# Selective scan on one core: products with C for two directions in one instruction, u for four rows, part of B's diagonals on GpSimd

## The chip, the cores and the metric

The kernel runs on one core of a Trainium2 chip. The core has five engines that run side by side, each with its own queue that it works through in order: TensorE (PE in the profile, with its weight loads as PEld), VectorE (DVE), ScalarE (ACT), GpSimd (POOL) and SyncE (SP, which here only issues transfers). The metric is the device time of one execution in microseconds (us), the median of several runs.

## The reference

Four layers are added to an image of 56 x 56 points with 128 channels, four images one after the other: a window attention layer with global attention and an MLP, a selective scan layer, a deformable convolution, and the first kind again. The change is in the second layer, whose core is a scan over the 3136 points in four orders (by rows, by columns, and both backwards), with 256 channels and 16 states for each channel:

```
def step(h, inp):
    u_i, d_i, b_i, c_i = inp
    dA = jnp.exp(d_i[..., None] * A)
    h = h * dA + (d_i * u_i)[..., None] * b_i[:, None, :]
    y = jnp.einsum('gdn,gn->gd', h, c_i)
    return (h, y)
...
x_t = jnp.transpose(xa, (0, 2, 1, 3)).reshape(b, L, D_INNER)
xs = jnp.stack([x_flat, x_t, jnp.flip(x_flat, 1), jnp.flip(x_t, 1)], axis=1)
...
dts4, Bp4, Cp4 = (rep4(dts), rep4(Bp), rep4(Cp))
```

The step sizes d, and B and C, are the same for the four directions at the same step number; only u differs. The four results are brought back to the image's order and added up.

## The kernel before

`run` takes the images in turn; for each, `mamba` first makes the convolved input `xa` and writes the step sizes and the rows of B and C to memory (`mamba_conv`), then runs `mamba_scan`, and then normalises, gates and projects (`mamba_out`). The change is inside `mamba_scan` alone, which stands four times in the span.

A **unit** of the scan is one line of 56 points in one direction, for 128 channels (half `j` of the 256) and all 16 states. On VectorE it is one scan instruction over 16 x 58 = 928 elements, where the two leading columns of every state carry the end of the line before. Units run in the order `(g, r, d)`: `g = 2s + j` is a pair of lines `s` for one half of the channels, `r` is the line in the pair, `d` the direction. There are 56 x 2 x 4 = 448 units in an image; eight units share a `g`.

Around each scan stand these steps, all recorded in an order written out by hand (`manual_schedule`): a loop over `u` (L1116) issues the fixed steps of each unit, and two lists, `soon` and `plan`, hold what `at(t, f)` has put at unit `t`. Each engine works its own instructions off in that order.

- `chunk` (L899): every 32 units, loads of step sizes and rows of B and C for four lines, 32 units ahead, and a split of the rows into a rounded part and a remainder.
- `mult` (L991): u times step size, `du`, on GpSimd, one instruction for each direction and two lines (112 elements).
- `high`, `low`, `low2` (L1004 to L1014): `du` in a rounded part (twice) and its remainder (twice), `dh`; ScalarE copies, GpSimd subtracts.
- `turn` and `keep` (L1016, L1021): TensorE transposes `dh`, ScalarE copies the result to `ut` (7 tiles).
- `b_rows` and `b_diag` (L943, L950): TensorE transposes the rows of B, VectorE spreads them along a diagonal mask into `dgb`, for one half line of 28 points (448 elements) in each instruction. The transposed rows lie in PSUM.
- `inputs` (L1041): TensorE multiplies `ut` with `dgb` into `dbu` in PSUM (2 buffers), one unit ahead of its scan.
- `zero` and `decays` (L996, L1000): the factors `da`; `inject` (L1057) and `save` (L1068): ScalarE copies the carry into `dbu` before a scan and out of `hs` after it.
- `scan` (L1061) writes `hs`; a tile `hs` holds two directions of one line, and there are three tiles.
- `c_spread` and `c_out` (L959, L970): C on all partitions, `cb`, for two lines.
- `weigh` (L1072): GpSimd multiplies `hs` by `cb` in place, one unit after the scan (896 elements).
- `add_up` (L1077): TensorE transposes the product and sums over the states, three units after the scan; `sum_out` (L1091): ScalarE copies a pair's sums to `ys` (6 tiles).
- `back` and `back_add` (L1095, L1102): TensorE turns the sums back, VectorE adds them to `ya`, at 14, 15 and 16 units from the start of the eight.

The order inside one unit `u` is: `save(u-1)`, `inputs(u+1)`, what `soon` holds, `weigh(u-1)`, `scan(u)`, `inject(u+1)`, `add_up(u-3)`, `sum_out` on every odd unit, and what `plan` holds.

Of the kernel before, what the change touches and what calls it, by code (L numbers as in the profile page):

```python
# [19 lines left out]
P = 128  # L20
HW = 56
# [19 lines left out]
NST = 16  # L41
SC = 224
# [36 lines left out]
class _Net:  # L79
# [795 lines left out]
    def mamba_scan(self, b, xa, ya, s1):  # L875
# [10 lines left out]
        with tc.tile_pool(name="ms", bufs=2) as sb, tc.tile_pool(name="ms_ps", bufs=2, space=PSUM) as ps, tc.manual_schedule():  # L886
# [6 lines left out]
            def at(t, f, plan=plan):  # L893
                plan.setdefault(t, []).append(f)
# [41 lines left out]
            def rows(s):  # L936

                m = made["r", s] = {}
                first = 16 * s
                src = made["c", s // 2]  # L940
                where = (s % 2) * 2 * HW

                def b_rows(r):  # L943
                    m["pb"] = bank("pbt")
                    for tb in range(2):
                        nc.tensor.transpose(
                            m["pb"][:TK, tb * NX : (tb + 1) * NX], src["xs"][:, (s % 2) * 4 + 2 * r + tb].rearrange("k g t -> k (g t)"), self.ident[:NX, :NX]
                        )

                def b_diag(r, tb):  # L950
                    t = m[r, tb] = sb.tile([TK, NST, TB], F32R, tag="dgb", name="dgb", bufs=8)
                    nc.vector.tensor_tensor(
                        t,
                        m["pb"][:TK, tb * NX + DTR : tb * NX + DTR + NST][:, :, None].to_broadcast([TK, NST, TB]),
                        dmask[:, None, :].to_broadcast([TK, NST, TB]),
                        ALU.mult,
                    )
# [12 lines left out]
                def c_out(k):  # L970
                    nc.scalar.copy(m["cb"][:, 4 * k : 4 * k + 4, :].rearrange("p n t -> p (n t)"), m.pop(("pc", k))[:, : 8 * HW])

                for r in range(2):
                    t = first - 16 + 8 * r
                    at(t, lambda r=r: b_rows(r))
                    for tb in range(2):
                        at(t + 1 + tb, lambda r=r, tb=tb: b_diag(r, tb))
                for k, t in enumerate((-10, -9, -2, -1)):
                    at(first + t + 1, lambda k=k: c_out(k))
                    at(first + t, lambda k=k: c_spread(k))  # L980

            def inputs_of(g):

                s, j = divmod(g, 2)
                m = made[g] = {}
                first = 8 * g - 15
                src = made["c", s // 2]
                dl = lambda: src["dl"][:, j, (s % 2) * 2 * HW : (s % 2 + 1) * 2 * HW].rearrange("p (r t) -> p r t", t=HW)
                flat = lambda t: t.rearrange("p d s g t -> p (d s) g t")

                def mult(d):  # L991
                    if d == 0:
                        m["du"] = sb.tile([P, 4, 2 * HW], F32, tag="du", name="du", bufs=1)
                    nc.gpsimd.tensor_tensor(m["du"][:, d, :].rearrange("p (r t) -> p r t", t=HW), dl(), self.direction(xa[:, j, :], d, 2 * s, 2), ALU.mult)

                def zero():  # L996
                    m["da"] = sb.tile([P, 2, NST, RW], F32, tag="da", name="da", bufs=3)
                    nc.gpsimd.memset(m["da"][:, :, :, 0:2], 0.0)

                def decays(n):  # L1000
                    for n in (n, n + 1):
                        nc.scalar.activation(m["da"][:, :, n, 2:], dl(), AF.Exp, scale=A[:, j, n : n + 1])  # L1002

                def high():  # L1004
                    m["dh"] = sb.tile([P, 4, 4, 4, TB], F32R, tag="dh", name="dh", bufs=1)
                    du = m["du"].rearrange("p d (s t) -> p (d s) t", t=TB)
                    nc.scalar.copy(flat(m["dh"])[:, :, 0:2, :], du[:, :, None, :].to_broadcast([P, 16, 2, TB]))

                def low():
                    du = m["du"].rearrange("p d (s t) -> p (d s) t", t=TB)  # L1010
                    nc.gpsimd.tensor_tensor(flat(m["dh"])[:, :, 2, :], du, flat(m["dh"])[:, :, 0, :].bitcast(F32), ALU.subtract)

                def low2():
                    nc.scalar.copy(flat(m["dh"])[:, :, 3, :], flat(m["dh"])[:, :, 2, :].bitcast(F32))  # L1014

                def turn(i):  # L1016
                    m["pt", i] = bank("pt")
                    for d in range(4):
                        nc.tensor.transpose(m["pt", i][:TK, d * P : (d + 1) * P], m["dh"][:, d, i].bitcast(F32).rearrange("p g t -> p (g t)"), self.ident)

                def keep(i):  # L1021
                    m["ut", i] = sb.tile([TK, 4, P], F32R, tag="ut", name="ut", bufs=7)
                    nc.scalar.copy(m["ut", i].rearrange("k d c -> k (d c)"), m.pop(("pt", i))[:TK, :])

                for d in range(4):
                    at(first + d, lambda d=d: mult(d))
                at(first + 4, zero)
                for i in range(8):
                    at(first + 5 + i, lambda i=i: decays(2 * i), soon)
                at(first + 5, high)  # L1030
                at(first + 6, low)
                at(first + 8, low2)
                for i in range(4):
                    at(first + 10 + i, lambda i=i: keep(i))
                    at(first + 9 + i, lambda i=i: turn(i))
# [5 lines left out]
            def inputs(u):  # L1041
                g, r, d = units[u]

                pu = ps.tile([P, 1024], F32, tag="dbu", name="dbu")
                pu = pu[:, 512 - UW // 2 : 512 + UW // 2].rearrange("p (n t) -> p n t", n=NST)
                for tb in range(2):
                    for h in range(2):
                        nc.tensor.matmul(  # L1048
                            pu[:, 8 * h : 8 * h + 8, 2 + tb * TB : 2 + (tb + 1) * TB],
                            lhsT=made[g]["ut", 2 * r + tb][:, d, :],  # L1050
                            rhs=made["r", g // 2][r, tb][:, 8 * h : 8 * h + 8, :].rearrange("k n t -> k (n t)"),
                            start=True,
                            stop=True,
                        )
                banks[u] = pu
# [13 lines left out]
                g, r, d = units[u]  # L1069
                nc.scalar.copy(carry[:, g % 2, d], pairs[u // 2][:, d % 2, :, HW:])  # L1070

            def weigh(u):  # L1072
                g, r, d = units[u]
                hs = pairs[u // 2][:, d % 2, :, 2:]
                nc.gpsimd.tensor_tensor(hs, hs, made["r", g // 2]["cb"][:, :, r * HW : (r + 1) * HW], ALU.mult)  # L1075

            def add_up(u):  # L1077

# [10 lines left out]
                    pairs.pop(q)  # L1089

            def sum_out(q):  # L1091
                backs[q] = sb.tile([YR, 2, P], F32, tag="ys", name="ys", bufs=6)
# [14 lines left out]
            for s in range(HW // 2):  # L1107
                if s % 2 == 0:
                    chunk(s // 2)
                rows(s)  # L1110
                for g in (2 * s, 2 * s + 1):
                    inputs_of(g)
                    at(8 * g + 14, lambda g=g: back(g))
                    for d in range(4):
                        at(8 * g + 15 + d // 2, lambda g=g, d=d: back_add(g, d))
            for u in range(-32, nu + 9):  # L1116
# [354 lines left out]
```

## Time and profile before

| What | us |
|---|---|
| median of 3 runs | 13266.81 |
| lowest and highest | 13265.99, 13270.98 |
| profiled execution | 13274.82 |
| its span, first to last instruction | 13273.0 |
| first to last scan, images 0 to 3 | 1016.4, 1016.8, 1015.9, 1016.8 |
| PE busy in the span | 11709.4 (88%) |
| DVE busy | 9579.6 (72%) |
| ACT busy | 7564.2 (57%) |
| POOL busy | 9942.5 (75%) |

In lists of groups, a line has the source line, engine, operation, the tile written and those read, the shapes (partitions x elements) and the count; then the busy time of all and the mean of one in ns, and last the idle time of the engine just before them with what ended it. In a timeline, a line has the start in us, the duration of what was merged, the engine and the work. Durations of neighbours on one engine overlap a little, so the distance from one start to the next tells what an instruction occupies. Ends of matmuls are modelled.

The scans take about 4067 us of the span together. Shares over the whole span mix stages with different limits, so the scan is read from a stretch inside it.

### The profile page before, as it was taken

What the parts mean: (1) busy time and instruction counts of PE and PEld (TensorE: products, weight loads), DVE (VectorE), ACT (ScalarE), POOL (GpSimd) and SP (SyncE); (2) the same over time, 40 slices, a digit from 0 to 9 for tenths busy, and PEclk for the clock granted to TensorE, in tenths of its full rate; (3) what the DMA queues carried; (4) which work ended last, traced back from release to release, by engine and by line L of the source; (5) the groups of instructions that cost most, each with busy time, mean ns of one, the idle gap of its engine ahead of it and who ended that gap; (6) DMA issues with size and microseconds to landing.
All of it is one profiled execution on the core that took longest, in us unless ns stands there. A gap on an engine that the chain in (4) does not pass through costs nothing. (4 is left out here: it accounts for less than half of the span.)

```text
span 13273.0 us, 218239 instructions
## 1 busy us (share of the span) xinstructions
PE 11709.4 (88%) x85716; PEld 7457.0 (56%) x85716; DVE 9579.6 (72%) x11831; ACT 7564.2 (57%) x19130; POOL 9942.5 (75%) x6852
## 2 busy tenths in 40 slices
PE   8999995799999999579999899956998989995799
PEld 4448883444544888344454488834445448883444
DVE  6649996665564999666566599966646649996664
ACT  5567772356556777235655677723565567772356
POOL 4949994488494999448849499944975949994497
PEclk9999997799999999779999999977999999997799
DMA  2000004200000000420000000042000000004200
GB/s 100 1 14 4 5 4 116 79 1 7 5 1 14 4 5 4 115 80 1 7 5 1 14 4 5 4 118 77 1 8 4 1 14 5 5 4 123 71 1 6
DMA packets 181178, 344.60 MB, mean 26 GB/s; under 512 B 20104, under 2 KB 101416, under 8 KB 180024
## 3 DMA queue, kind: packets, MB, share of 16 engines
q0 software_dynamic: 80640, 231.28, 6.2%
q1 hardware_dynamic: 99224, 97.83, 2.3%
q8 instruction: 678, 11.11, 0.3%
q14 instruction: 348, 2.85, 0.1%
q10 hardware_dynamic: 288, 1.53, 0.0%
HBM read 256.04 MB, written 74.52 MB: 25 GB/s over the span
## 5 line engine op out<-in xcount | busy, mean ns | idle before, releaser
L555 POOL TENSOR_TENSOR es<-es,e 128x896 f32<-128x896 f32 x2016 | 4159.6, 2088 | 132.6 <-ACT e L549 74.7
L350 DVE TENSOR_REDUCE mx<-pm 128x1 f32<-128x512 f32 (+1 forms) x4928 | 3059.2, 672 | 1404.8 <-PE pm L349 790.7
L549 ACT ACTIVATE e<-pst 128x448 f32<-128x448 f32 (+1 forms) x5600 | 2677.8, 544 | 1893.5 <-PE pst L547 1349.3
L1066 DVE TENSOR_TENSOR_SCAN hs<-da,dbu 128x928 f32<-128x928 f32 x1792 | 3633.5, 2071 | 54.3 <-ACT dbu L1059 29.0
L1075 POOL TENSOR_TENSOR hs<-hs,cb 128x896 f32<-128x896 f32 x1792 | 3484.2, 1961 | 26.9 <-ACT carry L1070 21.9
L349 PE MATMUL pm<-ks,qs 32*128 32x512 f32 (+1 forms) x9856 | 2912.8, 636 | 13.3 <-DVE nm L371 7.8
L547 PE MATMUL pst<-qs,ks 32*128 32x448 f32 x11200 | 2685.8, 548 | 0.0
L1084 PE MATMUL yt<-w_C,hs 128*116 128x128 f32 x14336 | 1866.1, 273 | 1.1 <-POOL hs L1075 1.1
L542 PE MATMUL pst<-nm,sel 32*128 32x448 f32 x5600 | 1639.2, 614 | 0.0
L1084 PEld LDWEIGHTS yt<-w_C,hs 128*116 128x116 f32 x14336 | 1570.8, 135 | 2.1 <-POOL hs L1075 2.1
L1048 PE MATMUL dbu<-dgb,ut 112*128 112x224 f32 x7168 | 1258.4, 298 | 268.9 <-DVE hs L1066 268.8
L571 PE MATMUL po<-e,va 128*32 128x448 f32 (+1 forms) x11200 | 1352.4, 551 | 0.1
L349 PEld LDWEIGHTS pm<-ks,qs 32*128 32x128 f32 x9856 | 925.9, 186 | 744.0 <-DVE mx L350 617.8
L1308 POOL DMA_INDIRECT g<-tab,idx x1008 | 940.3, 933 | 453.5 <-issue 429.7
L1048 PEld LDWEIGHTS dbu<-dgb,ut 112*128 112x128 f32 x7168 | 945.4, 192 | 534.4 <-DVE hs L1066 524.4
L1002 ACT ACTIVATE da<-dl,A 128x112 f32<-128x112 f32 x3584 | 1194.5, 383 | 0.1
L547 PEld LDWEIGHTS pst<-qs,ks 32*128 32x128 f32 x11200 | 1098.7, 185 | 102.3 <-issue 13.7
L1334 PE MATMUL pvt<-w_C,g 112*128 112x112 f32 x2016 | 400.1, 365 | 735.6 <-issue 610.6
L542 PEld LDWEIGHTS pst<-nm,sel 32*128 32x128 f32 x5600 | 571.0, 184 | 739.9 <-DVE mx L350 387.1
L1335 ACT COPY vt<-pvt 128x336 f32<-128x336 f32 x336 | 147.2, 438 | 1190.6 <-PE pvt L1334 1186.1
L1334 PEld LDWEIGHTS pvt<-w_C,g 112*128 112x128 f32 x2016 | 312.7, 201 | 827.4 <-issue 791.1
L1070 ACT COPY carry<-hs 128x32 f32<-128x32 f32 x1792 | 397.8, 222 | 624.4 <-DVE hs L1066 616.1
(230 smaller groups left out, 15785.8 us busy)
## 6 DMA issues: line engine op xcount, KB each, us to landing
tab<-zero SPq DMA_DIRECT2D x4, 6728.0 KB
g<-tab,idx POOLq DMA_INDIRECT x1008, 3.4
tab<-gt SPq DMA_DIRECT2D x32, 448.0 KB
dl_d<-dl SPq DMA_DIRECT2D x28, 448.0 KB
dl<-dl_d SPq DMA_DIRECT2D x56, 224.0 KB
tab<-gt SPq DMA_DIRECT2D x32, 336.0 KB
out_dram<-x SPq DMA_DIRECT2D x28, 224.0 KB
x<-in_x_dram SPq DMA_DIRECT2D x21, 224.0 KB
```

The source lines that it names most:

```text
L349: nc.tensor.matmul(pm[:, :m], lhsT=qs[head(h), q.start : q.start + P], rhs=ks[head(h), keys], start=True, stop=True)
L350: nc.vector.tensor_reduce(mx[:, home[i][1], h, kc : kc + 1], pm[:, :m], AX.X, ALU.max)
L542: nc.tensor.matmul(t[:, :CH], lhsT=self.sel[head(h), :], rhs=nm[head(h), part(qc)], start=True, stop=False)
L547: nc.tensor.matmul(t[:, :CH], lhsT=ks[head(h), k * KB : (k + 1) * KB], rhs=qs[head(h), part(qc)], start=False, stop=True)
L549: nc.scalar.activation(e[:nk, j, :], t[:nk, :CH], AF.Exp, scale=SCALE)
L555: nc.gpsimd.tensor_tensor(s, es[g - 1, p][:nk] if k == 1 else s, e[:nk], ALU.add)
L571: nc.tensor.matmul(m["po"][head(h), :CH], lhsT=va[:nk, k, head(h)], rhs=src(h)[:nk], start=(k == 0), stop=(k == NKB - 1))
L1002: nc.scalar.activation(m["da"][:, :, n, 2:], dl(), AF.Exp, scale=A[:, j, n : n + 1])
L1048: nc.tensor.matmul(pu[:, 8 * h : 8 * h + 8, 2 + tb * TB : 2 + (tb + 1) * TB], lhsT=made[g]["ut", 2 * r + tb][:, d, :], rhs=made["r", g // ...
L1066: nc.vector.tensor_tensor_scan(flat(pairs[u // 2][:, d % 2]), flat(made[g]["da"][:, r]), flat(banks.pop(u)), 0.0, ALU.mult, ALU.add)
L1075: nc.gpsimd.tensor_tensor(hs, hs, made["r", g // 2]["cb"][:, :, r * HW : (r + 1) * HW], ALU.mult)
L1084: nc.tensor.matmul(sums[q][:YR, e * P : (e + 1) * P], lhsT=hs[:, n, :], rhs=self.ident, start=(n == 0), stop=(n == NST // 2 - 1), is_trans ...
```

## The change

`weigh` is called once for a pair, on even units, for both directions of an `hs` tile (1792 elements, C repeated by a stride of zero); what follows it moves one unit later: `add_up` to four units after the scan, `sum_out` to even units, `back` and `back_add` by one. `mult` is made once for four lines (224 elements), earlier, into one tile for each half of the channels; `high` is two copies. `b_diag` covers a whole line (896 elements), and for two of each five lines it is done by GpSimd, from a copy of the transposed rows that ScalarE makes out of PSUM. `ut` has 6 tiles for 7, `ys` 5 for 6, `dgb` 4 of double size for 8.

```diff
-                def b_diag(r, tb):
-                    t = m[r, tb] = sb.tile([TK, NST, TB], F32R, tag="dgb", name="dgb", bufs=8)
-                    nc.vector.tensor_tensor(
-                        t,
-                        m["pb"][:TK, tb * NX + DTR : tb * NX + DTR + NST][:, :, None].to_broadcast([TK, NST, TB]),
-                        dmask[:, None, :].to_broadcast([TK, NST, TB]),
-                        ALU.mult,
+
+                mine = lambda r: (2 * s + r) % 5 in (1, 3)
+
+                def b_copy(r):
+                    if mine(r):
+                        pb = m["pb"]
+                        m["pb"] = sb.tile([TK, 2 * NX], F32, tag="pbc", name="pbc", bufs=1)
+                        nc.scalar.copy(m["pb"], pb[:TK, : 2 * NX])
+
+                def b_diag(r):
+                    t = m[r] = sb.tile([TK, 2, NST, TB], F32R, tag="dgb", name="dgb", bufs=4)
+                    b = m["pb"][:TK, : 2 * NX].rearrange("k (b n) -> k b n", b=2)[:, :, DTR : DTR + NST, None]
+                    (nc.gpsimd if mine(r) else nc.vector).tensor_tensor(
+                        t, b.to_broadcast([TK, 2, NST, TB]), dmask[:, None, None, :].to_broadcast([TK, 2, NST, TB]), ALU.mult
                     )
...
-                    for tb in range(2):
-                        at(t + 1 + tb, lambda r=r, tb=tb: b_diag(r, tb))
+                    at(t + 1, lambda r=r: b_copy(r))
+                    at(t + 2 if mine(r) else t + 1, lambda r=r: b_diag(r))
...
-                        m["du"] = sb.tile([P, 4, 2 * HW], F32, tag="du", name="du", bufs=1)
-                    nc.gpsimd.tensor_tensor(m["du"][:, d, :].rearrange("p (r t) -> p r t", t=HW), dl(), self.direction(xa[:, j, :], d, 2 * s, 2), ALU.mult)
+                        src["du", j] = sb.tile([P, 4, SC], F32, tag=f"du{j}", name="du", bufs=1)
+                    rows = lambda t: t.rearrange("p (r t) -> p r t", t=HW)
+                    nc.gpsimd.tensor_tensor(rows(src["du", j][:, d, :]), rows(src["dl"][:, j, :]), self.direction(xa[:, j, :], d, 2 * s, 4), ALU.mult)
+
+                def du():
+                    return src["du", j].rearrange("p d (r b t) -> p d r b t", r=2, t=TB)[:, :, s % 2]
...
-                    du = m["du"].rearrange("p d (s t) -> p (d s) t", t=TB)
-                    nc.scalar.copy(flat(m["dh"])[:, :, 0:2, :], du[:, :, None, :].to_broadcast([P, 16, 2, TB]))
+                    for k in range(2):
+                        nc.scalar.copy(m["dh"][:, :, :, k, :], du())
...
                 for d in range(4):
-                    at(first + d, lambda d=d: mult(d))
+                    if s % 2 == 0:
+                        at(first - 9 + 4 * j + 3 * d, lambda d=d: mult(d))
...
-            def weigh(u):
-                g, r, d = units[u]
-                hs = pairs[u // 2][:, d % 2, :, 2:]
-                nc.gpsimd.tensor_tensor(hs, hs, made["r", g // 2]["cb"][:, :, r * HW : (r + 1) * HW], ALU.mult)
+            def weigh(q):
+
+                g, r, d = units[2 * q]
+                hs = pairs[q][:, :, :, 2:]
+                cb = made["r", g // 2]["cb"][:, None, :, r * HW : (r + 1) * HW]
+                nc.gpsimd.tensor_tensor(hs, hs, cb.to_broadcast([P, 2, NST, HW]), ALU.mult)
...
-                if 0 <= u - 1 < nu:
-                    weigh(u - 1)
+                if u % 2 == 0 and 0 <= u - 2 < nu:
+                    weigh((u - 2) // 2)
                 if 0 <= u < nu:
                     scan(u)
                     if u + 1 < nu:
                         inject(u + 1)
                 elif u == -1:
                     inject(0)
-                if 0 <= u - 3 < nu:
-                    add_up(u - 3)
-                if 0 <= u - 4 < nu and u % 2 == 1:
-                    sum_out((u - 5) // 2)
+                if 0 <= u - 4 < nu:
+                    add_up(u - 4)
+                if 0 <= u - 5 < nu and u % 2 == 0:
+                    sum_out((u - 6) // 2)
```

More of the change, by code (lines that the diff above doesn't have):

```diff
@@ L1005, in high @@
                     m["dh"] = sb.tile([P, 4, 4, 4, TB], F32R, tag="dh", name="dh", bufs=1)
-                    du = m["du"].rearrange("p d (s t) -> p (d s) t", t=TB)
-                    nc.scalar.copy(flat(m["dh"])[:, :, 0:2, :], du[:, :, None, :].to_broadcast([P, 16, 2, TB]))
+                    for k in range(2):
+                        nc.scalar.copy(m["dh"][:, :, :, k, :], du())
                 def low():
-                    du = m["du"].rearrange("p d (s t) -> p (d s) t", t=TB)
-                    nc.gpsimd.tensor_tensor(flat(m["dh"])[:, :, 2, :], du, flat(m["dh"])[:, :, 0, :].bitcast(F32), ALU.subtract)
+                    nc.gpsimd.tensor_tensor(m["dh"][:, :, :, 2, :], du(), m["dh"][:, :, :, 0, :].bitcast(F32), ALU.subtract)
                 def low2():
@@ L1021, in keep @@
                 def keep(i):
-                    m["ut", i] = sb.tile([TK, 4, P], F32R, tag="ut", name="ut", bufs=7)
+                    m["ut", i] = sb.tile([TK, 4, P], F32R, tag="ut", name="ut", bufs=6)
                     nc.scalar.copy(m["ut", i].rearrange("k d c -> k (d c)"), m.pop(("pt", i))[:TK, :])
                 for d in range(4):
-                    at(first + d, lambda d=d: mult(d))
+                    if s % 2 == 0:
+                        at(first - 9 + 4 * j + 3 * d, lambda d=d: mult(d))
                 at(first + 4, zero)
@@ L1050, in inputs @@
                             lhsT=made[g]["ut", 2 * r + tb][:, d, :],
-                            rhs=made["r", g // 2][r, tb][:, 8 * h : 8 * h + 8, :].rearrange("k n t -> k (n t)"),
+                            rhs=made["r", g // 2][r][:, tb, 8 * h : 8 * h + 8, :].rearrange("k n t -> k (n t)"),
                             start=True,
@@ L1091, in sum_out @@
             def sum_out(q):
-                backs[q] = sb.tile([YR, 2, P], F32, tag="ys", name="ys", bufs=6)
+                backs[q] = sb.tile([YR, 2, P], F32, tag="ys", name="ys", bufs=5)
                 nc.scalar.copy(backs[q].rearrange("r e c -> r (e c)"), sums.pop(q)[:YR, : 2 * P])
@@ L1112, in mamba_scan @@
                     inputs_of(g)
-                    at(8 * g + 14, lambda g=g: back(g))
+                    at(8 * g + 15, lambda g=g: back(g))
                     for d in range(4):
-                        at(8 * g + 15 + d // 2, lambda g=g, d=d: back_add(g, d))
-            for u in range(-32, nu + 9):
+                        at(8 * g + 16 + d // 2, lambda g=g, d=d: back_add(g, d))
+            for u in range(-32, nu + 11):
                 if 0 <= u - 1 < nu:
```

## The prediction

> **What bounds the kernel now.** I read three views: the totals of one undisturbed scan stretch, the groups of instructions, and the timeline of GpSimd and VectorE, because only an order of starts shows what an instruction really occupies.
>
> The first view is the table by stretch (columns: the stretch, then length, PE, PEld, DVE, ACT and POOL busy, clock, DMA). Four such scan stages stand in the span, one for each image.
>
> ```profile
> 1030.00:2000.00 970.00, 901.54 (x7338) 813.17 (x7337) 960.61 (x743) 704.92 (x2415) 968.47 (x758) 1.00 0.02 5
> ```
>
> POOL (968.47 of 970.00) and DVE (960.61) are both full; PE's ends are modelled, and ACT has room. The groups, in full-length lists by engine:
>
> ```profile
> L1066 DVE TENSOR_TENSOR_SCAN hs<-da,dbu 128x928 f32<-128x928 f32 x1792 | 3633.5, 2071 | 54.3 <-ACT dbu L1059 29.0 <-POOL hs L1075 2.6
> ...
> L1105 DVE TENSOR_TENSOR ya<-ya,pyb 128x112 f32<-128x112 f32 x896 | 278.1, 310 | 31.2 <-PE pyb L1100 15.5
> L952 DVE TENSOR_TENSOR dgb<-pbt,w_C 112x448 fp32r<-112x448 f32 x448 | 268.3, 600 | 27.1 <-PE pbt L946 27.1
> ...
> L1178 DVE TENSOR_TENSOR xc<-xc,z 128x896 f32<-128x896 f32 x28 | 30.6, 1093 | 26.8 <-ACT xc L1177 26.8
> ```
>
> ```profile
> L555 POOL TENSOR_TENSOR es<-es,e 128x896 f32<-128x896 f32 x2016 | 4159.6, 2088 | 132.6 <-ACT e L549 74.7
> L1075 POOL TENSOR_TENSOR hs<-hs,cb 128x896 f32<-128x896 f32 x1792 | 3484.2, 1961 | 26.9 <-ACT carry L1070 21.9 <-PE dbu L1048 1.5
> ...
> L994 POOL TENSOR_TENSOR du<-dl,xa 128x112 f32<-128x112 f32 x896 | 423.5, 474 | 2.1 <-DMA dl<-dl_d 1.8
> L1011 POOL TENSOR_TENSOR dh<-du,dh 128x448 fp32r<-128x448 f32 x224 | 259.4, 1158 | 30.0 <-ACT dh L1007 30.0
> ...
> L275 POOL TENSOR_TENSOR pz<-s,m 64x784 f32<-64x784 f32 x128 | 191.8, 1498 | 748.2 <-DVE m L272 500.2 <-PE ln_pv L156 243.5
> ...
> L660 POOL TENSOR_TENSOR x<-x,x 128x448 f32<-128x448 f32 x56 | 63.4, 1132 | 401.0 <-PE ln_pc L147 393.7 <-DVE ln_sq L668 7.3
> ```
>
> The weighing's idle is 26.9 us in four scans: POOL hardly ever waits. Now the starts (start, duration, engine, work), POOL and then DVE:
>
> ```profile
> 1528.62 0.16 POOL L998 MEMSET da<- 128x64 f32 x1
> 1528.72 3.85 POOL L1075 TENSOR_TENSOR hs<-hs,cb 128x896 f32<-128x896 f32 x2
> 1532.51 1.15 POOL L1011 TENSOR_TENSOR dh<-du,dh 128x448 fp32r<-128x448 f32 x1
> 1533.61 3.86 POOL L1075 TENSOR_TENSOR hs<-hs,cb 128x896 f32<-128x896 f32 x2
> 1537.43 0.43 POOL L994 TENSOR_TENSOR du<-dl,xa 128x112 f32<-128x112 f32 x1
> 1537.82 1.94 POOL L1075 TENSOR_TENSOR hs<-hs,cb 128x896 f32<-128x896 f32 x1
> ```
>
> ```profile
> 1539.71 0.60 DVE L952 TENSOR_TENSOR dgb<-pbt,w_C 112x448 fp32r<-112x448 f32 x1
> 1540.22 9.99 DVE L1066 TENSOR_TENSOR_SCAN hs<-da,dbu 128x928 f32<-128x928 f32 x5
> 1550.13 0.66 DVE L1105 TENSOR_TENSOR ya<-ya,pyb 128x112 f32<-128x112 f32 x2
> ```
>
> Start to start, a weighing occupies 1.90 us (3.79 / 2), a small du product 0.41 (0.39 here, 0.44 for the turned directions), the remainder L1011 1.10, the memset 0.10, and xs (L921) 0.62 once in four rounds. A scan occupies 1.985, a dgb 0.51, a ya about 0.285 (four in 1.14). I call 8 units (one g) a round. POOL: 8 x 1.90 + 4 x 0.41 + 1.10 + 0.10 + 0.16 = 18.20 us. DVE: 8 x 1.985 + 2 x 0.51 + 1.14 = 18.04. From the first scan's start to the last's, image 0 takes 1016.4 us (1004.0 to 2020.4), 55.9 rounds of 18.19. Both engines set the pace together, so a gain needs both to fall.
>
> **The change part by part.** *Paired weighing (1792 elements).* No row shows that length. Lower bound: the slope of L275 (with one operand repeated) from the fixed part, 1942 + 896 x 1.69 ns, less the 0.04 that neighbours overlap: 3.42 us. Upper: no fixed cost at all, 2 x 1.90 = 3.80. L660 to L555 gives 2.13 ns per element and so 1132 - 448 x 2.13 = 0.17 us of fixed cost, of which some 0.13 shows from start to start; I take 3.65, nearest to the weighing's own row. The Trainium skill ("GPSIMD Engine Reference", section 3.1) puts an elementwise product at about 2.6 cycles an element and gives 4497 ns at 2048 elements; an estimate by it is 3.9 us for 1792, no gain at all, and the sum would then be worse than my upper bound. By that page's 1.2 GHz, L1075's 1942 ns for 896 is 2.6 cycles too, while L660 against L555 shows a fixed part; no run here shows the longer product.
>
> *du for four rows.* 224 elements: 0.41 + 112 x 2.13 ns = 0.65, plus some for turned reads, 0.68 (between 0.62 and 0.80); two a round for four. Saved: 1.64 - 1.36 = 0.28.
>
> *Diagonals.* 22 of 56 in an image go to POOL: 896 elements with both operands repeated, between 0.17 + 896 x 1.69 ns = 1.68 by L275's slope and 2.05 by L555; I take 1.70, by L275, the row with a repeated operand. The other 34 are one instruction of 896 on DVE: 1.09 in L1178's row, less overlap, 0.98 (0.95 to 1.03) for 2 x 0.51. ACT gains 22 copies (about 0.23 like carry) and pays 2 x 0.57 for 0.94 us in splitting dh: 17 us an image on an engine with 265 us free in the stretch. Without that cover these 17 us would count. A copy stands a unit ahead of its diagonal, which is itself behind a weighing on POOL, so that wait costs nothing; behind it stands the next weighing.
>
> *Queues.* SP's transfers stay. The du products come 9 units earlier, still 8 units (18 us) behind their load, which landed 3.1 us after issue (988.02 to 991.10). PE issues the same matmuls; fewer spare ut and ys tiles still leave their readers ahead of their next writers.
>
> *Sums.* POOL after: 4 x 3.65 + 2 x 0.68 + 1.36 = 17.32 in a round, 19.02 with a diagonal, mean 17.99. DVE: 8 x 1.985 + 1.14 = 17.02, 18.00 with a diagonal, mean 17.62. If lateness averaged out, POOL would set 55.9 x 17.99 = 1006 us, 11 below now.
>
> *Where the lateness goes.* It does not average out freely. Now a product is finished 1.94 us after its start and read by PE three units on; counting the 0.33 us to start behind a scan, the 0.47 of PE's inputs and 1.1 us that PE can be late, POOL may lag 2 x 1.985 + 0.47 + 1.1 - 1.94 - 0.33 = 3.3 us. After, the product starts only when both scans are done, takes 3.69 (its full duration), is read two units later, and the third pair after it overwrites its tile: add_up of the second half ends 0.47 + 1.12 + 0.1 into a unit of 1.985, and PE's unit of inputs, transposes and turn (0.47 + 0.84 + 0.46) leaves 0.2 more, so 0.5 of lateness. The lag allowed is 3.97 + 0.47 + 0.5 - 3.69 - 0.33, about 1 to 1.2 us, and 1.14 more where it falls in units 0 and 1 of a round, in which DVE also adds ya: 2.4.
>
> Units 2 to 7 of a round: DVE 6 x 1.985 = 11.91; POOL 3 x 3.65 + 1.02 + 1.36 = 13.33, or 15.03 with a diagonal, so it falls behind by 1.42 or 3.12 us. In units 0 and 1 POOL has 3.65 + 0.34 and DVE 5.11, or 6.09 with its own diagonal: POOL regains 1.12 or 2.10. (Before, the lag was 6 x 1.90 + 1.23 + 1.36 - 12.42 = 1.57, within 3.3.) With 1.2 allowed, DVE waits 3.12 - 1.2 = 1.92 in each of 22 rounds and about 0.27 in 34: 22 x 18.94 + 34 x 18.27, about 1036 us in 55.9 rounds. With 2.4 allowed and the rest of a lag carried into the next round, five rounds (two with POOL's diagonal) cost waits of 0.72, 0.30, 1.02, 0.30 and 0, in sum 2.34, 11.2 times an image, on DVE's 55.9 x 17.62 = 985: 1011. I take the middle, 1023. The scan that waits is next late for its carry, and so is the pair four units on.
>
> *Ends.* At the start the first dh remainder stands behind five long du products and xs: about 1.2 us. At the end the last pair's product is 1.75 longer and both transposes (0.84 more) follow it: 2.6. Together 4 us an image.
>
> The sum is 4 x (1023 - 1016.4 + 3.8) = 41.6. The profiled execution took 13274.82 us (span 13273.0, 1.8 around it), 8 above the median of 13266.81; by it 13316, by the median 13308.
>
> **Rivals.** *Lateness averages out.* For it: POOL waits so little now. Against: only three pairs of hs. Then 1006 + 4 against 1016.4, -26 over four images: 13241; with the pair at 3.42, POOL's mean is 17.07 and DVE sets 985: (985 + 4 - 1016.4) x 4 = -110: 13157. The case spans both; about 13200. It decides from a pair under about 3.55: 0.10 less takes 0.30 from the lag of units 2 to 7 and allows 0.10 more, so 22 waits fall by 0.40, 9 us an image.
>
> *Nothing saved by length.* The pair at 3.80 puts 0.60 on each round: at best 55.9 x 18.59 = 1039, with the ends 27 an image: 13374. For it: 1942 ns is a plain rate per element.
>
> *Gain and lumps cancel.* 1011 + 4 is 1.4 below now: 13261. For it: most lag falls due in the long units 0 and 1.
>
> **How the numbers follow.** Forecast 0.38, averaging 0.28, no saving 0.16, cancelling 0.18. This kernel's measurement tells 0.2% (27 us) from no change. The forecast's own range is half way to its bounds, 1017 to 1030 us an image: 13284 to 13337; the faster case gives 0.28, the cancelling one and a small edge 0.20 of same, the rest is slower, 0.52. The range 13180 to 13395 leaves out the full VectorE bound and the worst pile of prices.
>
> **What would show it.** The products' mean beside 3.69; POOL's idle ahead of them rising from 7 us an image to 20 or more, released by the scan or its carry copy; DVE idle ahead of scans, released by the injected carry or by yt, above 14 an image; diagonals on POOL near 1.75; first-to-last scan 1023. A product under 3.55 us, or POOL idle with DVE full, would make this wrong.

## The result: 0.6% slower, and the profile after

The changed kernel took 13356.4 us (median of 4 runs, 13352.47 to 13360.17) beside 13268.9 us for the kernel before on the same chip (13265.99 to 13278.78): a ratio of 1.0062 [1.0049, 1.0075]. Its profiled execution took 13352.47 us (span 13350.7), 77.7 more than the profiled execution before.

All of that lies in the four scan layers. In each image the layer is cut here at five starts on VectorE: the last step-size instruction of `mamba_conv` (L816), the first scan, the last scan, the last addition to `ya`, and the last addition to `x`; the mean of four images, in us:

| Stage | before | after | more |
|---|---|---|---|
| ahead of the first scan | 28.2 | 31.1 | 2.8 |
| first to last scan | 1016.5 | 1030.1 | 13.6 |
| last scan to last `ya` | 8.2 | 11.8 | 3.6 |
| from there to the end of the layer | 81.6 | 82.6 | 1.0 |

These add up to 84.2 over four images; the rest of the program came out 6.5 shorter.

The groups of the profile page after, in the form shown of before (line, engine, operation, tiles, shapes, count; then busy, mean ns; then idle ahead and what ended it):

```profile
L1078 DVE TENSOR_TENSOR_SCAN hs<-da,dbu 128x928 f32<-128x928 f32 x1792 | 3602.6, 2068 | 200.8 <-PE yt L1098 112.2
L1089 POOL TENSOR_TENSOR hs<-hs,cb 128x1792 f32<-128x1792 f32 x896 | 3316.7, 3708 | 143.3 <-ACT carry L1082 141.4
```

The full lists by engine, the smaller GpSimd and VectorE groups:

```profile
L1003 POOL TENSOR_TENSOR du<-dl,xa 128x224 f32<-128x224 f32 x448 | 326.1, 729 | 12.7 <-DMA dl<-dl_d 12.7
...
L962 POOL TENSOR_TENSOR dgb<-pbc,w_C 112x896 fp32r<-112x896 f32 x88 | 153.7, 1746 | 5.0 <-ACT pbc L957 5.0
```

```profile
L1119 DVE TENSOR_TENSOR ya<-ya,pyb 128x112 f32<-128x112 f32 x896 | 284.0, 317 | 46.0 <-PE pyb L1114 30.3
L962 DVE TENSOR_TENSOR dgb<-pbt,w_C 112x896 fp32r<-112x896 f32 x136 | 147.0, 1081 | 24.0 <-PE pbt L946 24.0
```

The products of `hs` and C fell from 3484.2 us to 3316.7, but their idle time rose from 26.9 to 143.3, released by the carry copy, which a scan releases; the scans' idle rose from 54.3 to 200.8, and 112.2 of it is now released by TensorE's `yt`, the reader of the product. Each engine waits for the other in turn. The table of one scan stretch shows both sides (columns: the stretch; length, PE, PEld, DVE, ACT, POOL busy, clock, DMA share, GB/s):

```profile
1035.00:2005.00 970.00, 886.88 (x7254) 815.32 (x7252) 932.27 (x664) 697.60 (x2463) 943.54 (x448) 0.99 0.02 5
```

Before, a stretch of the same length had DVE busy 960.61 and POOL 968.47. Now both have room (38 and 26 us), and yet the stage is longer. That is the sign of lateness, not of a full engine.

### The profile page after: what moved, and what is told of

Same layout as the page of the kernel before. It is cut to its first block, busy times and chain, and to the rows that moved or that the text cites. A ratio compares the mean times of both kernels' runs of the same rounds, so it can differ in the third digit from the quotient of the medians.

```text
span 13350.7 us, 218239 instructions
## 1 busy us (share of the span) xinstructions
PE 11677.5 (87%) x85716; PEld 7497.8 (56%) x85716; DVE 9514.5 (71%) x11519; ACT 7568.3 (57%) x19442; POOL 9908.9 (74%) x5596
## 5 line engine op out<-in xcount | busy, mean ns | idle before, releaser
L1078 DVE TENSOR_TENSOR_SCAN hs<-da,dbu 128x928 f32<-128x928 f32 x1792 | 3602.6, 2068 | 200.8 <-PE yt L1098 112.2
L1089 POOL TENSOR_TENSOR hs<-hs,cb 128x1792 f32<-128x1792 f32 x896 | 3316.7, 3708 | 143.3 <-ACT carry L1082 141.4
L1098 PE MATMUL yt<-w_C,hs 128*116 128x128 f32 x14336 | 1900.4, 276 | 191.0 <-POOL hs L1089 189.2
L275 POOL TENSOR_TENSOR pz<-s,m 64x784 f32<-64x784 f32 x128 | 192.0, 1500 | 752.9 <-DVE m L272 504.9
```

What stands on the lines that cost most here:

```text
L1078: nc.vector.tensor_tensor_scan(flat(pairs[u // 2][:, d % 2]), flat(made[g]["da"][:, r]), flat(banks.pop(u)), 0.0, ALU.mult, ALU.add)
L1089: nc.gpsimd.tensor_tensor(hs, hs, cb.to_broadcast([P, 2, NST, HW]), ALU.mult)
L1098: nc.tensor.matmul(sums[q][:YR, e * P : (e + 1) * P], lhsT=hs[:, n, :], rhs=self.ident, start=(n == 0), stop=(n == NST // 2 - 1), is_trans ...
```

## The experiments

The whole program took about 13490 us on some chips and 13270 on others, the kernel before included; so ratios stand only between kernels that shared a chip. The scan stage is compared across chips, since a scan's mean was 2065 to 2071 ns and a pair product's 3705 to 3718 ns in every run; the kernel before was profiled on one chip only. A stage's figure is from one profiled execution, whose four images lie within 4 us of each other. All diffs are against the changed kernel unless said otherwise. First the table of all, then the readings; "scan" is first to last scan, mean of four images.

| Kernel | scan us | ahead of it | last scan to last `ya` | time against before |
|---|---|---|---|---|
| before | 1016.5 | 28.2 | 8.2 | 1 |
| after | 1030.1 | 31.1 | 11.8 | 1.0062 [1.0049, 1.0075] |
| e1, diagonals a unit earlier | 1026.3 | 31.1 | 11.3 | 1.0048 [1.0031, 1.0064] |
| e2, no diagonals on GpSimd | 1010.7 | 31.0 | 11.3 | 0.9989 [0.9980, 0.9999] |
| e3, du as before, 3 `hs` tiles | 1029.9 | 28.3 | 11.8 | 1.0068 [1.0051, 1.0084] |
| e4, the same, 4 `hs` tiles | 1037.1 | 28.8 | 11.8 | 1.0069 [1.0052, 1.0085] |
| e5, e4 and `add_up` two units later | 1019.4 | 28.2 | 10.9 | 13295 by 13279 |
| e6, pair products, long diagonals | 1010.0 | 28.6 | 11.8 | 13257 by 13279 |
| e7, all of the change, with 4 `hs` tiles and e5's order | 1007.8 | 31.9 | 10.9 | 0.9972 [0.9960, 0.9983] |
| e8, e7 with one of five diagonals | 1009.1 | 31.6 | 10.9 | 0.9979 [0.9969, 0.9989] |
| e9, before with diagonals on GpSimd | 1048.8 | 28.3 | 8.2 | 13601 by 13492 |
| e10, before with du and long diagonals | 1013.3 | 30.8 | 8.2 | 13477 by 13492 |
| e11, e7 trimmed | 1005.6 | 28.9 | 10.4 | 0.9967 [0.9955, 0.9979] |

Rows with two times set one execution beside the median of before on the same chip, which itself lay between 13253.81 and 13297.65 for e5 and e6, and between 13479.28 and 13501.51 for e9 and e10; they are read by their stages.

### Which part costs: e2, e9, e6, e10

e2 takes the diagonals off GpSimd and leaves the rest of the change:

```diff
-                mine = lambda r: (2 * s + r) % 5 in (1, 3)
+                mine = lambda r: False
```

> The changed kernel with all diagonals on VectorE (one instruction of 896 elements a round). GpSimd has 17.32 us a round, VectorE 18.00. Theory A: every round is like those that had VectorE's diagonal, lag 1.4 us against 1.2 to 2.4 allowed, so 18.0 to 18.3 us a round, first-to-last scan 1006-1022 us, time 13255-13315. Rival B: VectorE alone sets it, 1006, with the ends 13255. Rival C: the waits stay, about 36 us an image on top of VectorE's 1006, so 1040 and 13390.

Measured: 1010.7 us, 19.4 an image less than after. The full list by engine of e2, the scans and then the products:

```profile
L1078 DVE TENSOR_TENSOR_SCAN hs<-da,dbu 128x928 f32<-128x928 f32 x1792 | 3591.4, 2067 | 43.3 <-POOL dh L1022 28.0 <-PE yt L1098 6.1 <-issue 0.2
```

```profile
L1089 POOL TENSOR_TENSOR hs<-hs,cb 128x1792 f32<-128x1792 f32 x896 | 3315.1, 3705 | 201.4 <-ACT carry L1082 199.3 <-POOL da L1010 0.4
```

The scans' waits for `yt` went from 112.2 us to 6.1, and GpSimd is idle 201.4: now VectorE sets the pace. The instructions that e2 gives back to VectorE, 22 of 0.98 us an image, are 21.6 us more work on it, and still the stage is shorter by 19.4. So in the changed kernel the diagonals on GpSimd cost about 41 us an image of lost time against 22 of saving.

e9 goes the other way: the kernel before, with the long diagonals and two of five on GpSimd, and nothing else (the diff is against the kernel before).

```diff
+                mine = lambda r: (2 * s + r) % 5 in (1, 3)
...
+                    at(t + 1, lambda r=r: b_copy(r))
+                    at(t + 2 if mine(r) else t + 1, lambda r=r: b_diag(r))
```

> The kernel before with one part of the change: long diagonals, two of five on GpSimd. Products stay single and du for two lines. GpSimd 18.20 + 0.39 x 1.70 = 18.87 us a round, VectorE about 17.7. Theory A (GpSimd's sum is paid in full once it cannot lag further): 55.9 x 18.87 = 1055 us from first to last scan, ends as before (28 and 8). If instead the diagonals cost only because of the pairs' short reach, single products, which may lag 3.3 us, should hide them: 1016-1022.

Measured: 1048.8, 32 an image above before. The table of a stretch of e9:

```profile
1040.00:2000.00 960.00, 877.24 (x7026) 791.56 (x7024) 900.28 (x643) 677.57 (x2331) 960.00 (x747) 0.99 0.02 5
```

POOL is busy for 960.00 of 960.00 and DVE has 60 us of room. The theory of a full engine said 1055, the one of a short reach 1016 to 1022. Here it is a full engine: 22 diagonals at 1.70 are 37 us more on an engine that had nothing left, a little over the 32 measured.

e6 keeps the pair products and puts the long diagonals on VectorE, with du as before; e10 is the kernel before with the new du, and the long diagonals on VectorE.

```diff
-                mine = lambda r: (2 * s + r) % 5 in (1, 3)
+                mine = lambda r: False
...
-                    if s % 2 == 0:
-                        at(first - 9 + 4 * j + 3 * d, lambda d=d: mult(d))
+                    at(first + d, lambda d=d: mult(d))
```

> Of the change, only the paired product (with add_up one unit later) and the long diagonals, all on VectorE; du is made for two lines at its old place. GpSimd 17.6 us a round by 3.69 for a pair (17.76), VectorE 18.00. Theory A: little lag, VectorE sets 1006-1014 us, start as before the change (28 us), end about 11 (8 before): within 0.2% of the kernel before. If pairing by itself made the waits, the scan would stay near 1030.

> The kernel before with du for four lines and long diagonals, all on VectorE; products stay single. GpSimd 18.20 - 0.28 = 17.92 us a round, VectorE 18.0-18.14: 1008-1014 us from first to last scan, a start of 31 us (28 before), an end of 8.

Measured: 1010.0 and 1013.3, so 6.5 and 3.2 an image below before, and 1010.7 for both parts together (e2). The gains don't add, since VectorE is the limit in all three (busy for 950 to 954 of 960 us of the stage): its round is 8 x 1.985 + 0.98 + 1.14 = 18.00, which is 1006 us in 55.9 rounds. Each part also brings a loss at one end: the new du 2.6 to 2.8 us ahead of the first scan (e2, e10; at most 0.6 in e3 to e6), the pair product 2.7 to 3.6 after the last (absent in e9 and e10). Pairing by itself made no waits in the scan: e6 has it and is shorter than before. They came with the diagonals on a GpSimd that could not lag.

### What makes the waits: e1, e3, e4, e5

I had two explanations of the 38 us of waits: the place of GpSimd's lump in a round, and how far GpSimd may lag before someone waits, which I had put down to the three `hs` tiles. e1 moves the lump one unit, away from the rest of the busy stretch:

```diff
-                    at(t + 2 if mine(r) else t + 1, lambda r=r: b_diag(r))
+                    at(t + 1, lambda r=r: b_diag(r))
```

> The changed kernel with one edit: GpSimd's diagonals are issued one unit earlier, ahead of the pair product of units 0 and 1 and not behind it. GpSimd's work is the same, 17.99 us a round. Theory A (lateness: GpSimd's lump of 1.70 us falls due in the light units 2 to 7, where three pair tiles allow a lag of only 1.2 to 2.4 us): the lump now lies in units 0 and 1, where GpSimd otherwise has about 1.1 us to spare, so the first-to-last scan falls from 1030 to 1008-1018 us an image and the time to 13270-13310. Rival B (GpSimd's total work sets the pace): unchanged, 1030 and 13356. Rival C (the later add_up and back on TensorE, fewer ut and ys tiles): unchanged too.

Measured: 1026.3, 3.8 below after and well short of 1008 to 1018. A place one unit earlier is worth little: that theory was a miss, and the time is nearer to the rivals' 1030.

e3 and e4 test the tiles. A fourth `hs` tile needs memory, so both have du as before and 5 `ut` tiles, and they differ in one number:

```diff
-                    pairs[u // 2] = sb.tile([P, 2, NST, RW], F32, tag="hs", name="hs", bufs=3)
+                    pairs[u // 2] = sb.tile([P, 2, NST, RW], F32, tag="hs", name="hs", bufs=4)
```

> The changed kernel with du made for two lines again (four products of 112 elements a round), which frees room, and with ut at 5 tiles: the base for the next run. GpSimd's sum is 18.27 us a round. Theory A: 1032-1042 us from first to last scan, 13365-13400. Rival B: 1030 x 18.27 / 17.99 = 1046, 13420. Rival C: above 1030 by what the tile of ut costs.

> The run before with one edit: four hs pair tiles for three. Theory A: GpSimd may lag a pair more (about 4 us), its lumps average out and it sets 55.9 x 18.27 = 1021 us or a few more; 12 to 20 us an image less than the run before, time 13310-13340. Rival B: as the run before. Rival C: as the run before.

Measured: 1029.9 with three tiles, below all three forecasts: 0.28 us more work on GpSimd in each round lengthened nothing, so GpSimd's work was not what set 1030. And 1037.1 with four tiles: no gain, so the theory of e4 missed too. The scans in the full lists by engine, of e3 and then of e4:

```profile
L1074 DVE TENSOR_TENSOR_SCAN hs<-da,dbu 128x928 f32<-128x928 f32 x1792 | 3600.9, 2068 | 202.7 <-PE yt L1094 106.5 <-ACT dbu L1067 48.8 <-ACT carry L1078 25.0
```

```profile
L1074 DVE TENSOR_TENSOR_SCAN hs<-da,dbu 128x928 f32<-128x928 f32 x1792 | 3599.8, 2067 | 192.2 <-ACT dbu L1067 187.1
```

The wait did not go; its name changed, from the reader that frees the tile (`yt`) to the injected carry, which follows the scan's inputs. The timeline of TensorE in the changed kernel shows both at one wait (start, duration, engine, work; in brackets the idle before and what ended it):

```profile
1356.47 0.71 PE L1060 MATMUL dbu<-dgb,ut 112*128 112x224 f32 x4
1358.85 1.94 PE L1098 MATMUL yt<-w_C,hs 128*116 128x128 f32 x8 [1.67 <-POOL hs L1089]
1360.43 1.08 PE L972 MATMUL pcb<-x,ident 104*128 104x112 f32 x4
1361.32 1.15 PE L1060 MATMUL dbu<-dgb,ut 112*128 112x224 f32 x4
1362.26 1.07 PE L1098 MATMUL yt<-w_C,hs 128*116 128x128 f32 x8
```

And GpSimd and VectorE at the same time:

```profile
1345.43 7.38 POOL L1089 TENSOR_TENSOR hs<-hs,cb 128x1792 f32<-128x1792 f32 x2
1352.75 1.75 POOL L962 TENSOR_TENSOR dgb<-pbc,w_C 112x896 fp32r<-112x896 f32 x1
1354.46 0.68 POOL L1003 TENSOR_TENSOR du<-dl,xa 128x224 f32<-128x224 f32 x1
1355.09 3.71 POOL L1089 TENSOR_TENSOR hs<-hs,cb 128x1792 f32<-128x1792 f32 x1
```

```profile
1348.39 11.97 DVE L1078 TENSOR_TENSOR_SCAN hs<-da,dbu 128x928 f32<-128x928 f32 x6
1363.47 2.09 DVE L1078 TENSOR_TENSOR_SCAN hs<-da,dbu 128x928 f32<-128x928 f32 x1 [3.11 <-PE yt L1098]
```

The lump of diagonal and du pushes the product to 1355.09 and its end to 1358.80. TensorE works its queue in order: `add_up` of that pair stands ahead of the next unit's `inputs` (1361.32), so the late product holds up matmuls that do not need it. The scan behind them starts at 1363.47, 3.11 us late. ScalarE had injected its carry by 1362.69, and the second `yt` group, which frees its tile, ended at 1363.33. So with three tiles the tile came last, but only 0.64 us behind the inputs, and a fourth tile can take no more than that off this wait. In e4 a wait at the same place of a round, its first unit, shows the inputs last:

```profile
1273.82 0.70 PE L1056 MATMUL dbu<-dgb,ut 112*128 112x224 f32 x4
1276.55 1.09 PE L1094 MATMUL yt<-w_C,hs 128*116 128x128 f32 x8 [2.03 <-POOL hs L1085]
...
1277.98 1.15 PE L1056 MATMUL dbu<-dgb,ut 112*128 112x224 f32 x4
```

```profile
1279.45 2.09 DVE L1074 TENSOR_TENSOR_SCAN hs<-da,dbu 128x928 f32<-128x928 f32 x1 [1.74 <-ACT dbu L1067]
```

The inputs stand behind a `yt` that waits 2.03 us for its product. e5 is e4, with `add_up` and what follows two units later.

```diff
-                if 0 <= u - 4 < nu:
-                    add_up(u - 4)
-                if 0 <= u - 5 < nu and u % 2 == 0:
-                    sum_out((u - 6) // 2)
+                if 0 <= u - 6 < nu:
+                    add_up(u - 6)
+                if 0 <= u - 7 < nu and u % 2 == 0:
+                    sum_out((u - 8) // 2)
```

> The kernel with two-line du and four hs tiles, with one edit: add_up stands six units after its scan in TensorE's order, not four (sum_out two units later too). Theory A, mended (the tiles were not the limit: add_up stands ahead of the next inputs in TensorE's queue, so a late product holds up inputs, carry and scan): GpSimd may now lag two units more, some 4 us; the waits ahead of scans go and GpSimd's sum of 18.27 us a round sets 1021-1027 us from first to last scan, with under 12 us an image of idle ahead of the products (25 in the run with four tiles). Rival B (a product waits for both its scans, so GpSimd idles whatever TensorE does): 1037 as before.

Measured: 1019.4, 18 below e4 and just under the forecast. The products in e4 and then in e5, and the table of a stretch of e5:

```profile
L1085 POOL TENSOR_TENSOR hs<-hs,cb 128x1792 f32<-128x1792 f32 x896 | 3321.0, 3707 | 99.5 <-ACT carry L1078 98.5
```

```profile
L1085 POOL TENSOR_TENSOR hs<-hs,cb 128x1792 f32<-128x1792 f32 x896 | 3331.1, 3718 | 33.1 <-ACT carry L1078 33.0
```

```profile
1040.00:2000.00 960.00, 886.82 (x7232) 813.49 (x7230) 927.89 (x665) 691.94 (x2400) 959.22 (x556) 0.99 0.02 5
```

POOL is at 959.22 of 960.00: with room to lag, GpSimd is simply full. This needs both, the fourth tile and the later `add_up`. The order alone cannot be had with three tiles: the scan of unit u opens the tile that held units u-6 and u-5, and `add_up` six units after its scan would read them only behind that scan.

### All of the change, with room: e7, e8, e11

e7 has the change's own pairs, du and diagonals, with e5's order. The memory comes from one `ut`, one `ys` and one `dgb` tile less, with the diagonals spaced to match and the split of the chunk's rows a little later:

```diff
-                at(first - 22, high)
-                at(first - 20, low)
-                at(first - 18, low2)
+                at(first - 19, high)
+                at(first - 18, low)
+                at(first - 17, low2)
...
-                    t = first - 16 + 8 * r
+                    t = first - 16 + 12 * r
...
-                    pairs[u // 2] = sb.tile([P, 2, NST, RW], F32, tag="hs", name="hs", bufs=3)
+                    pairs[u // 2] = sb.tile([P, 2, NST, RW], F32, tag="hs", name="hs", bufs=4)
```

> The changed kernel, all its work, with more reach: four hs tiles, add_up six units after the scan, and room for that found in dgb (3 tiles, the second line's diagonal four units later), ut (5) and ys (4). Theory A: GpSimd's work of 17.99 us a round (18.15 with 3.69 for a pair) sets 1006-1016 us instead of 1030, ratio to the kernel before 0.996-1.001. Rival B: 1030, ratio 1.006.

Measured: 1007.8, 22 below the changed kernel with the same work, and 13244.7 us by 13279.05: 0.9972 [0.9960, 0.9983]. With room to lag, the diagonals on GpSimd cost no more than they save (e2, without them and without the room, had 1010.7). The fewer `ut` and `ys` tiles, the third explanation on record, did not make the waits: e7 has one less of each still, and a stage 22 us shorter.

e8 is e7 with `mine` for one line in five:

```diff
-                mine = lambda r: (2 * s + r) % 5 in (1, 3)
+                mine = lambda r: (2 * s + r) % 5 == 1
```

> As the run before, with one of five diagonals on GpSimd. GpSimd 17.32 + 0.16 + 0.2 x 1.70 = 17.82, VectorE 17.02 + 0.8 x 0.98 = 17.80 us a round: 996-1006 us from first to last scan by theory A, with the longer ends (+5.5 us an image) 0.993-0.998 of the kernel before. Rival B: 1015-1022, ratio about 1.002.

Measured: 1009.1, no better than e7 and above 996 to 1006: a miss. A stretch of it:

```profile
1040.00:2000.00 960.00, 872.77 (x7310) 808.22 (x7310) 948.12 (x679) 695.75 (x2454) 933.64 (x439) 1.00 0.02 5
```

VectorE is about as full as before the change: in image 0 it is busy for 996.5 us and idle for 12.8 in gaps ahead of scans and `ya`, beside 10.5 in the kernel before. The forecast began at 55.9 x 17.82 = 996, a sum of work with no gaps. The list of waits of e8 from 1140 to 2000 us (who waits for whom, us in total, times, longest) has one on TensorE that the changed kernel, with four `dgb` tiles, does not have:

```profile
PEld pt L1030 <- DVE dgb L962: 25.9, 18, 1.4
```

TensorE's transposes of `dh`, behind which the inputs stand, wait for a diagonal that VectorE makes behind a scan. What it costs the stage is not shown; e7 has such waits too. e11 has e7's tiles and its later `add_up`, but leaves the split of the chunk where it was, puts the second diagonal nine units behind the first, takes one line in three, and shortens both ends: the first lines' du at their old place, and the last pair's product as two of the old length.

```diff
-                mine = lambda r: (2 * s + r) % 5 in (1, 3)
+                mine = lambda r: (2 * s + r) % 3 == 1
...
-                    t = first - 16 + 8 * r
+                    t = first - 16 + 9 * r
...
-                        at(first - 9 + 4 * j + 3 * d, lambda d=d: mult(d))
+                        at(first - 9 + 4 * j + 3 * d if s else first + d, lambda d=d: mult(d))
...
-                if u % 2 == 0 and 0 <= u - 2 < nu:
+                if u % 2 == 0 and 0 <= u - 2 < nu - 2:
                     weigh((u - 2) // 2)
+                if nu - 2 <= u - 1 < nu:
+                    weigh_one(u - 1)
```

> The change with reach and without its longer ends: four hs tiles, add_up six units after the scan, room from dgb (3 tiles, the second line's diagonal one unit later), ut (5), ys (4); the first chunk's du products at their old units; the last pair's product in two halves; one of three diagonals on GpSimd. GpSimd 17.22 + 0.57 = 17.8 us a round, VectorE 18.14 - 0.33 = 17.8. Theory A: 995-1003 us from first to last scan, start 28-29, end 8.5-10, ratio to the kernel before 0.993-0.997.

Measured: 13445.26 us by 13491.66, 0.9967 [0.9955, 0.9979], faster than the kernel before by 46 us. That wait of TensorE for a diagonal is gone from its list; which of the edits took it away was not tried singly. The scan stage, 1005.6, is less short than forecast (995 to 1003, which again begins at a sum of work, 55.9 x 17.8), and the end, 10.4, a little longer. A stretch of it:

```profile
1035.00:2005.00 970.00, 896.41 (x7402) 825.40 (x7401) 950.32 (x680) 702.74 (x2478) 959.52 (x453) 1.00 0.02 5
```

VectorE is busy for 950.32 and GpSimd for 959.52 of 970.00: what is left of waiting on either is about 2% and 1%.

## Why the prediction was right, and where it was wrong

*Direction and order of size.* The prediction asked for lateness that doesn't average out, and that is what the runs show. The time it named was 48 us low by the medians: inside its wide range, but above its own case of 13284 to 13337. The direction came for the reason given; how near the waits came to 38 us an image was partly luck, as said below. By the profiled executions it is 36 (13352.5 for 13316); the other 12 are that the profiled execution before lay 8 above its median and the one after 4 below. The 36 are 28 and 14 that the next points name, less the 6.5 by which the rest of the program came out shorter.

*Prices: right.* Two products in a row start 7.32 us apart (1345.43 to 1352.75), 3.66 each beside 3.65; du 0.63 (1354.46 to 1355.09) where it is not turned, beside 0.68; a diagonal on GpSimd 1.71 (1352.75 to 1354.46) beside 1.70. The long diagonal on VectorE has a mean of 1.08 beside the 1.09 it was worked out from. By the "GPSIMD Engine Reference" of the Trainium skill (section 3.1) the longer product was estimated at 3.9 us and would have saved nothing; this case's 3.71 is 5% below that, and the measurement decides. The fixed part that two halves share shows: twice 1942, the median of the short product before, less the mean of 3708 is 176 ns recorded.

*The mean of these prices: right.* The prediction said that GpSimd's rounds would give 1006 us if lateness averaged out. e7, which does all of that work with room to lag, took 1007.8. The rival "lateness averages out" described a kernel with another order in TensorE's queue.

*The size of the waits: right ahead of the scans, short by the gaps ahead of `ya` and some work.* The forecast of 1023 was VectorE's 985 of work and 38 of waits. In image 0 of the changed kernel the waits ahead of the scans are 37.9, and another 4.8 stand ahead of `ya`, as the full list for that stretch shows:

```profile
L1078 DVE TENSOR_TENSOR_SCAN hs<-da,dbu 128x928 f32<-128x928 f32 x441 | 886.6, 2068 | 37.9 <-PE yt L1098 24.4 <-ACT da L1014 3.3 <-ACT cb L978 3.1
L1119 DVE TENSOR_TENSOR ya<-ya,pyb 128x112 f32<-128x112 f32 x216 | 68.4, 317 | 4.8 <-PE pyb L1114 1.1
```

985 + 37.9 + 4.8 is 1027.7; measured 1030.1. The last 2.4 is work: VectorE was busy for 987.4 us of that stage. The step that failed is "*on DVE's 55.9 x 17.62 = 985*": a worked-out sum of work was set against a measured stage. By the same prices the kernel before has 55.9 x 18.04 = 1008 and took 1016.4 in image 0, with 10.5 us of gaps ahead of its scans and `ya`; the old side of the subtraction held such gaps and the new one did not. The stage was missed by 7.1 an image, 28 over four: in image 0, 4.8 ahead of `ya` and 2.4 of work. The agreement of 37.9 with 38 is in part luck: 38 was the middle of 26 and 51, chosen without a reason to prefer it. And the 51 rests on a sum that does not come out: 3.97 + 0.47 + 0.5 - 3.69 - 0.33 is 0.92, not 1 to 1.2; with it the upper figure is 1050 for 1036.

*The cause of the limit: wrong in part.* "*The third pair after it overwrites its tile*" named the `hs` tiles, and the profile after does show `yt`, which frees a tile, as the releaser of most of the waits. What the prediction lacked is the limit right behind it: `add_up` stands ahead of the next inputs in an in-order queue, 0.64 us behind the tile in the wait shown. So e4, with a fourth tile, gained nothing, and the later place in TensorE's order, which the fourth tile makes possible, took 18 us off.

*The round's long units: wrong.* "*And 1.14 more where it falls in units 0 and 1*" made much of the place within the round. e1 moved the lump and gained 3.8 us.

*Ends: too small.* Forecast 1.2 at the start and 2.6 at the end, measured 2.8 and 3.6, and 1.0 behind them: 7.4 for 3.8 an image, 14 over four. At the end, a wait was costed at its own length, and it made the matmuls behind it longer too. TensorE at the end of image 0's scan:

```profile
2030.93 3.32 PE L1098 MATMUL yt<-w_C,hs 128*116 128x128 f32 x16 [1.98 <-POOL hs L1089]
...
2037.82 2.98 PE L1163 MATMUL pm<-ya,w_C 128*128 128x448 f32 x4 [1.54 <-DVE ya L1119]
```

Just ahead of it sixteen `yt` took 1.96, and before the change the same four `pm` took 1.74. In images 1 and 2 there was no such slow stretch, and the end was 10.9: 2.7 longer than before, beside the 2.6 forecast. Images 0 and 3 had 12.6.

*What the prediction said it would see.* The products' idle of 20 us or more an image: 143.3 / 4 = 36. Idle ahead of scans above 14: 200.8 / 4 = 50, of which the start of each scan layer is 11.7 in image 0. Diagonals near 1.75 us: 1.746. First to last scan at 1023: 1030.1.

## What to carry to other kernels

When two engines are both full and work in a ring, an average of their work says little: here work of 17.99 us a round took 1030 us with little room to run late and 1008 with more. Count how many units late a result may be before the first wait, and where. In this kernel that room was set by the order in the consumer's queue as much as by the number of tiles, and more tiles alone gained nothing: put reads of a late result behind work that doesn't need it, and give the tiles to match. And set a worked-out stage only against a worked-out stage, never against a measured one.

## What the hardware showed that I had not expected

*A short wait of TensorE can slow what follows it.* The table by stretch around the wait of 1.67 us shown above, in stretches of 3.41 us (TensorE's busy time is the second number behind the stretch, the clock the third from the end):

```profile
1355.51:1358.92 3.41, 1.74 (x15) 1.35 (x13) 3.41 (x3) 2.17 (x7) 3.41 (x2) 1.00 0.01 2
1358.92:1362.33 3.41, 3.41 (x17) 3.41 (x18) 1.45 (x1) 1.72 (x5) 3.41 (x3) 0.50 0.00 0
```

TensorE was busy for half of the first stretch, and through the second the granted clock was 0.50; in that time eight `yt` took 1.94 us (1.04 at other times), four `pcb` 1.08 (0.63) and four `dbu` 1.15 (0.71), some 1.8 us more, and VectorE's wait behind them was 3.11. Behind the first 12 us of image 0's scan, six of the groups of eight `yt` were that slow (1.54 to 1.94), none before the change and none in e2. It doesn't follow every such wait: before the change, waits of 1.54 and 1.82 us at the end of the scan left `pm` at 1.74 and `pz` at 1.77. The half-clock stretches of this trace all begin whole multiples of 3.413 us apart, so where a wait falls in that grid may decide; that is not shown. The Trainium skill ("TensorE: Matmul & The Clock Gate", Part 1) has the half rate, and a window of about 3.4 us that runs freely; the 0.50, its length and the grid agree. It also says that a whole idle window of that length is needed; here TensorE was idle for only half of one, and the measurement decides: a wait much shorter than the window can cost the half clock.

The half clock by itself does not account for the length of the stage: behind its first 12 us an image's scan had 22 us of it in the changed kernel and 12 in e3, and the stages are 1030.1 and 1029.9.

*Freeing one of two limits moved the wait.* e4 against e3 differs in one tile and was 7 us an image longer in the scan. The gaps ahead of scans shrank by 2.6 us an image, from 39.2 to 36.6, but those ahead of `ya` grew from 3.7 to 13.7. The row of `ya` in e4 (44.8 us of idle in e3):

```profile
L1115 DVE TENSOR_TENSOR ya<-ya,pyb 128x112 f32<-128x112 f32 x896 | 284.9, 318 | 84.7 <-PE pyb L1110 68.7
```

`pyb` stands behind the same late `add_up` in TensorE's queue. The half clock was longer as well, 30 us an image for 12, and the two are not separated. The whole times don't differ within the intervals (1.0069 and 1.0068): the profiled execution of e3 was the shortest of its four and that of e4 the longest, 12 us below and 13 above their medians, so how much of the 7 us other executions of e4 show is open.
